# Seven block products for q, k, v and gates of seven sequences, and a first phase in three stages

## The chip, the cores and the metric

The kernel runs on one core of a Trainium2 chip. The metric is the device time of one execution in microseconds (us); a kernel's time is the median of its runs. Engines are named as the profile names them: PE is TensorE's matmul, PEld its weight load, DVE is VectorE, ACT is ScalarE, POOL is GpSimd, SP is SyncE, whose queue issues most DMAs.

## What is computed

Eight sequences of 1024 tokens of width 512, all float32. Cut to what matters:

```python
xn = layernorm(x)
q = xn @ Wq                                  # 512 -> 128
gate = softmax(xn @ Wg, axis=-1)             # 512 -> 3
for i in range(3):
    k, v = xn @ Wk[i], xn @ Wv[i]            # 512 -> 128 each
    w = decay[i] ** max(t_diff - 1, 0) * causal
    blended += gate[..., i:i+1] * ((q @ k.T * w) @ v)
s = blended @ Wo * out_scale
g = silu(ffn(xn))          # gate, up, down: weights lut[idx], 1376 wide inside
out = x + s * g
```

In the kernel's layout the causal mask runs backwards in time: a token attends to those behind it, so chunks of 128 tokens are worked from the last to the first, with a running state that decays from chunk to chunk.

## The kernel before, in words

It has two phases. Phase 1 (`phase_1`, to 604.8 us of the span) does the attention up to `blended` for each sequence, stores normalized tokens and sums of their blocks (`xs_d`) for phase 2, and builds the feed-forward weights from the table of 16 values (`ffn_weights`). Phase 2 is the feed-forward part, on weights and tokens that it loads back; its big products already go by seven products of blocks instead of eight, at two levels.

Phase 1 is written as Python generators that a loop steps by hand: for each sequence `b` eight steps `k`, each with three sections. `keep_order` (L26) then fixes that order for PE, DVE, ACT and POOL, so every engine works its instructions in the order in which they are traced; SP's queue is fixed only for the first steps. `tick` and `defer` put a DMA's issue some sections later. The generators:

- `project(b)`: for each of eight chunks load x (L335), statistics on ACT with a power on POOL (L350 to L353; on DVE for sequence 0, L343 to L347), normalize (L361 or L358), four transposes to `xnT` (`pt`, L366), copied by ACT (L367). Values and gate logits of a chunk are four matmuls of 387 columns (`pv`, L373); queries and keys of half a sequence are four times four matmuls of 512 columns (`pq`, L410). Each result is copied once by ACT (L376, L413). The softmax of the gates goes through DRAM (`gT_d`) and comes back broadcast to all partitions (`ga`). At the end DVE forms four sums of token blocks (`ts`, L467), and the features of the first half are still being made while the next sequence starts (`ending`).
- `chunks(b-1)`: for each chunk, from the last: keys are transposed (`pk`, L507) and scaled by ACT (`ks`, L510); `gated` multiplies gates and queries on DVE (`qa`, in place in `ga`, L491) and then by a decay table on POOL (`qb`, L495); scores (`psc`, L516), times the decay mask on DVE (`pr`, L518); state update (`pu`, L524) and output (`po`, L538), copied by ACT into `bl` (L539). The state is copied by ACT (L543) and scaled in PSUM (L550).
- `ffn_weights`: 16 jobs and more of a table lookup on DVE, 19 instructions on 1024 columns each (bits L197, index L200, leaves L204, selects L221), then block sums on POOL (L249 to L253, L267 to L273), then stores to `wgu_d`, `quad_d`, `wd_d`. The lookup's result lies in a tile `wgu` with two buffers: a job's first leaf (L204 `wgu<-`) waits until the job two before has let go of its buffer.

PSUM has eight banks: four in the pool `p_a` (`pt`, `pv`, `pq`), three in `p_c` (`pk`, `psc`, `po`), one in `p_r` (`pu`). A tile's buffer comes free when all that read it are done.

Within a step of the loop the order is: first section `pk` and its scalings, then `pt` and the statistics; second section `pq` and the softmax, then `gated`, `psc` and `pr`; third section `pv`, then `pu`, `po` and the state. `build_some` puts up to six pieces of `ffn_weights` (a piece is most often one VectorE instruction) between them.

Of the kernel before, what the change touches and what calls it, by code (L numbers as in the profile page):

```python
# [9 lines left out]
F32 = mybir.dt.float32  # L10
# [7 lines left out]
P = 128  # L18
# [19 lines left out]
def recurrent_block(ctx: ExitStack, tc, x, wq, wk, wv, wo, wg, decay_logits, out_scale, lut, gidx, uidx, didx, out):  # L38
# [18 lines left out]

    nc = tc.nc
# [12 lines left out]
    NQ = NO // 4  # L71
    EPS = 1e-5
# [20 lines left out]
    def more_weights(wvg_sb, wqk_sb):  # L93
        nc.scalar.dma_start(out=wvg_sb[:, :, NI * D :], in_=wg.rearrange("(c p) d -> p c d", p=P))
# [51 lines left out]
    def tables():  # L146
# [31 lines left out]
        for step, first in ((1, 0), (0, P)):  # L178
            back = small.tile([P, NI, P], F32, name="back", tag="back", bufs=2)
            nc.sync.dma_start(  # L180
                out=back, in_=bass.AP(pow_d.tensor, pow_d.offset + first, [[step, P], [2 * P, NI], [1, P]])
            )
            backs.append(back)
# [42 lines left out]
    def ffn_weights(build, pool, pair_pool):  # L226
# [5 lines left out]

        upper = []

        def gate_up(o):
# [19 lines left out]
            defer(3, lambda: nc.sync.dma_start(out=wgu_d[o], in_=wide))  # L255
            if o >= 2 * NK:
                return
            if o % 2 == 0:
                upper.append(w[:, 1:])
                return  # L260
            up, low = upper.pop(), w[:, 1:]
            to = quad_d[o // 4][:, :, o // 2 % 2, :].rearrange("p k (t m) -> p k t m", m=P)
            pair = pair_pool.tile([P, 7, 4, P], F32, name="pair", tag="pair")
            nc.sync.dma_start(out=to[:, :, 0:2, :], in_=up)
            defer(3, lambda: nc.sync.dma_start(out=to[:, :, 2, :], in_=low[:, :, 1, :]))
            b21, b22, b11, b12 = low[:, :, 0], low[:, :, 1], up[:, :, 0], up[:, :, 1]
            nc.gpsimd.tensor_tensor(pair[:, :, 0], b21, b22, ALU.add)  # L267
            yield
            nc.gpsimd.tensor_tensor(pair[:, :, 1], pair[:, :, 0], b11, ALU.subtract)
            yield  # L270
            nc.gpsimd.tensor_tensor(pair[:, :, 2], b11, b21, ALU.subtract)
            yield
            nc.gpsimd.tensor_tensor(pair[:, :, 3], b12, pair[:, :, 1], ALU.subtract)  # L273
            defer(4, lambda: nc.sync.dma_start(out=to[:, :, 3:7, :], in_=pair))
# [34 lines left out]

    def warm_up(n):  # L310

        warm = p_a.tile([P, P], F32, name="warm", tag="a")
# [3 lines left out]
    def project(b, pools, sides, kept):  # L316

        xp, xnp, tp, att = pools
        wvg_sb, wqk_sb = sides
        xnT = xnp.tile([P, NV, T], F32, name=f"xnT{b}", tag="xnT")
        mean, rstd, shift = (small.tile([P, NC], F32, name=f"{k}{b}", tag=k) for k in ("mean", "rstd", "shift"))
        v_sb = att.tile([P, NC, NI * D + NI], F32, name=f"v{b}", tag="v")
        gt = v_sb[:, :, NI * D :]
        qT, kT = {}, {}
        gates = []
        kept[b] = (v_sb, gates, qT, kT)  # L330
        xts = {}

        def load(c):
            xts[c] = xp.tile([P, V], F32, name=f"x{b}_{c}", tag="x")
            nc.sync.dma_start(out=xts[c], in_=x[b, ts(c, P), :])  # L335

        def statistics(c):

            m, r = mean[:, c : c + 1], rstd[:, c : c + 1]
            if b == 0:  # L340
                st = small.tile([P, 6], F32, name=f"st{b}_{c}", tag="st")
                mv = small.tile([P, 2], F32, name=f"mv{b}_{c}", tag="mv")
                nc.vector.bn_stats(st, xts[c])  # L343
# [4 lines left out]
            else:  # L348
                junk = small.tile([P, V], BF16, name=f"junk{b}_{c}", tag="junk", bufs=1)
                nc.scalar.activation(junk, xts[c], AF.Copy, scale=-1.0 / V, accum_out=m)  # L350
                nc.scalar.activation(junk, xts[c], AF.Square, bias=m, accum_out=r)  # L351
# [3 lines left out]
        def normalize(c):  # L355
# [757 lines left out]
```

## Time and profile before

| | |
|---|---|
| median of 3 runs | 2160.95 us (2160.52 to 2160.99) |
| the profiled execution's own time | 2158.71 us |
| its span, first to last instruction | 2156.9 us |
| granted TensorE clock | 1.000 |
| first matmul of phase 2's products (L687) | 608.3 us |
| transposes of sequences 0 to 7 begin at | 6.0, 46.3, 120.5, 194.8, 270.7, 344.9, 419.1, 493.3 us |
| DMA | 316.8 MB, 147 GB/s over the span |

How to read the page: "busy" is the time in which an engine had an instruction under way, "xcount" the number of instructions. A group's line has the source line, the engine and operation, the tiles as out<-in, the shape, the count, then busy time and the mean of one in ns, then the engine's idle time just before them with what ended it. In the timeline each line is a run of like instructions: start, length, engine, line, tiles, shape, count, and in brackets the idle time before with its releaser. The view by windows gives, for a stretch of time, its length and the busy time of PE, PEld, DVE, ACT and POOL with their counts, then the granted clock, DMA share and GB/s.

### The profile page before, as it was taken

Reading aid. Unit: us, or ns where it says so; the run is one execution under the profiler, and the core shown is the slowest. Engines: PE = TensorE matmul, PEld = TensorE weight load, DVE = VectorE, ACT = ScalarE, POOL = GpSimd, SP = SyncE. Lnnn points to the kernel's source line nnn. Section 1 sums busy time; section 2 is a strip of 40 time slices with the busy share of each in tenths; the row PEclk is TensorE's granted clock in tenths of the full one; section 3 lists DMA queues with packets and bytes.
Section 4 is the critical chain, followed back from the end, with each engine's and each line's share of the span. In section 5 each row is a group of like instructions: output and inputs, shape, how many; then the busy total and the mean of one; then the engine's idle time right before and its main releaser. Section 6 shows DMA issues by size and latency. Waiting matters only on the chain.

```text
span 2156.9 us, 26203 instructions
## 1 busy us (share of the span) xinstructions
PE 2147.4 (100%) x9486; PEld 1647.1 (76%) x9486; DVE 1158.4 (54%) x1701; ACT 863.9 (40%) x1900; POOL 979.8 (45%) x902
## 2 busy tenths in 40 slices
PE   9999999999999999999999999999999999999998
PEld 5666666666668778778878887887788688778876
DVE  6888687678645435534543453354345435533543
ACT  3666666666334214413431441243144124413521
POOL 2554545444244553634455452455435353634442
PEclk9999999999999999999999999999999999999999
DMA  8776654545374434434442443345244334434411
GB/s 193 192 196 177 205 199 153 186 147 162 114 297 154 145 106 150 141 115 138 150 155 96 145 149 117 130 154 169 75 152 149 130 117 154 129 119 149 156 57 54
DMA packets 145943, 316.83 MB, mean 147 GB/s; under 512 B 50867, under 2 KB 76214, under 8 KB 144790
## 3 DMA queue, kind: packets, MB, share of 16 engines
q1 hardware_dynamic: 135974, 290.50, 41.7%
q0 software_dynamic: 7728, 23.86, 3.0%
q8 instruction: 75, 1.23, 0.2%
q10 hardware_dynamic: 2112, 0.79, 0.1%
q14 instruction: 54, 0.44, 0.1%
HBM read 233.98 MB, written 81.14 MB: 146 GB/s over the span
## 4 chain that ended last, share of the span: by engine, by line
PE 98%; POOL 1%; issue 0%; ACT 0%; DVE 0%; DMA 0%; POOLq 0%
PE s L737 32%; PE ds L976 22%; PE pq L410 10%; PE pv L373 8%; PE sE L737 5%; PE fs L687 4%; PE po L538 4%; PE ds L987 2%; PE ps L998 2%; PE psc L516 2%; PE pu L524 2%; PE fsE L687 2%; PE pt L366 1%; PE pk L507 1%; PE sE L780 1%; PE s L780 1%
## 5 line engine op out<-in xcount | busy, mean ns | idle before, releaser
L737 PE MATMUL s<-xs,wq 128*128 128x256 f32 x3192 | 715.1, 379 | 0.0
L737 PEld LDWEIGHTS s<-xs,wq 128*128 128x128 f32 x3192 | 605.6, 190 | 94.1 <-issue 7.0
L976 PE MATMUL ds<-wd,s 128*128 128x256 f32 x1280 | 286.7, 379 | 0.0
L976 PEld LDWEIGHTS ds<-wd,s 128*128 128x128 f32 x1280 | 243.2, 190 | 33.1
L410 PE MATMUL pq<-xnT,wqk_sb 128*128 128x512 f32 x512 | 230.3, 592 | 0.0
L976 PE MATMUL ds<-wd,h 128*128 128x256 f32 x960 | 222.9, 379 | 0.0
L976 PEld LDWEIGHTS ds<-wd,h 128*128 128x128 f32 x960 | 182.3, 190 | 52.5 <-issue 27.1
L831 POOL TENSOR_TENSOR u<-u,e 128x512 f32<-128x512 f32 x64 | 79.8, 1268 | 276.1 <-DVE u L827 276.1
L760 DVE TENSOR_TENSOR s<-s,e 128x512 f32<-128x512 f32 x133 | 93.0, 700 | 202.2 <-ACT s L759 202.2
L373 PE MATMUL pv<-wvg_sb,xnT 128*128 128x387 f32 x512 | 177.5, 488 | 0.0
L1001 POOL TENSOR_TENSOR gx<-gx 128x512 f32<-128x512 f32 x63 | 80.3, 1274 | 184.3 <-DVE gx L999 183.6
L410 PEld LDWEIGHTS pq<-xnT,wqk_sb 128*128 128x128 f32 x512 | 92.4, 190 | 92.1 <-issue 91.8
L764 DVE TENSOR_TENSOR sE<-s,e 128x512 f32<-128x512 f32 x133 | 93.0, 699 | 102.6 <-PE s L737 102.6
L737 PE MATMUL sE<-xs,wq 128*128 128x256 f32 x532 | 136.5, 379 | 0.0
L352 POOL TENSOR_SCALAR rstd<-rstd 128x1 f32<-128x1 f32 x56 | 26.8, 479 | 238.2 <-ACT junk L351 237.6
L373 PEld LDWEIGHTS pv<-wvg_sb,xnT 128*128 128x128 f32 x512 | 92.7, 190 | 54.3 <-issue 1.9
L755 ACT COPY e<-sE 128x512 f32<-128x512 f32 x133 | 77.8, 585 | 136.1 <-PE sE L737 136.1
L671 POOL TENSOR_TENSOR xs<-xs 128x1792 f32<-128x1792 f32 (+1 forms) x38 | 127.9, 3380 | 1.0
L1017 ACT ACTIVATE gx<-ds 128x256 f32<-128x256 f32 x32 | 12.3, 383 | 285.9 <-PE ds L987 285.9
L759 ACT COPY s<-s 128x512 f32<-128x512 f32 x133 | 75.8, 570 | 96.6 <-PE s L737 96.6
L748 ACT COPY s<-s 128x512 f32<-128x512 f32 x133 | 75.8, 570 | 95.8 <-PE s L737 92.1
L737 PEld LDWEIGHTS sE<-xs,wq 128*128 128x128 f32 x532 | 101.1, 190 | 13.7
(169 smaller groups left out, 3298.2 us busy)
## 6 DMA issues: line engine op xcount, KB each, us to landing
wq<-quadd SPq DMA_DIRECT2D x112, 896.0 KB, 4.4
xs<-xsd SPq DMA_DIRECT2D x8, 3584.0 KB, 11.9
wq<-quadd SPq DMA_DIRECT2D x42, 448.0 KB, 3.8
x<-in_x SPq DMA_DIRECT2D x64, 256.0 KB, 5.9
xsd<-ts SPq DMA_DIRECT2D x8, 2048.0 KB, 7.0
gx<-in_x SPq DMA_DIRECT2D x64, 256.0 KB, 2.7
out<-gx POOLq DMA_DIRECT2D x63, 256.0 KB, 2.3
ga<-gTd SPq DMA_DIRECT2D x16, 768.0 KB, 4.9
```

Source lines behind the costliest of these rows:

```text
L373: nc.tensor.matmul(pv, lhsT=xnT[:, v, ts(c, P)], rhs=wvg_sb[:, v, :], start=(v == 0), stop=(v == NV - 1))
L410: nc.tensor.matmul(pq, lhsT=wqk_sb[:, v, ts(j, D)], rhs=xnT[:, v, ts(hf, U)], start=(v == 0), stop=(v == NV - 1))
L538: nc.tensor.matmul(po, lhsT=lh, rhs=rh, start=(n == 0), stop=(n == len(prods) - 1))
L671: nc.gpsimd.tensor_tensor(o, x1, x2, ALU.subtract)
L687: nc.tensor.matmul(ps, lhsT=w[:, 2 * W_OF[k] + n, :m], rhs=xs[:, X_OF[k], 2 * n : 2 * n + 2, :], start=start and n == 0, stop=stop and n == 1,
L737: nc.tensor.matmul(self.t[n][:, ts(a, H)], lhsT=self.w[:, a, (0, 1, 6, 2, 3, 4, 5)[i - 1], :], rhs=self.xs[:, X_OF[self.ks[a]], D_OF[i], : ...
L755: nc.scalar.copy(self.e, self.t[3])
L760: nc.vector.tensor_tensor(self.t[1], self.t[1], self.e, ALU.add)
L764: nc.vector.tensor_tensor(self.t[3], self.t[2], self.e, ALU.add)
L831: nc.gpsimd.tensor_tensor(o[:, n], o[:, n], other[:, n], ALU.add)
L976: nc.tensor.matmul(ps, lhsT=lhs[k][:, n, :], rhs=wd_sb[n][:, ts(D_OF[k], H)], start=start and n == 0, stop=stop and n == NK - 1, skip_grou ...
L1001: (nc.vector if end else nc.gpsimd).tensor_tensor(g, g, xr, ALU.add)
```

## The change

For sequences 1 to 7, values with gates and queries with keys are computed by seven products of blocks in place of eight (`nodes`), from four sums of token blocks and four sums of weight blocks. The value weights are padded from 387 to 388 columns and cut in two halves of 194 (`HG`). Each of four nodes a sequence (two for values, each with products of four matmuls of 194 columns, two for queries and keys, each with products of two matmuls of 512) has four PSUM roles with a bank each (`p_a` now has one buffer for each of four tags); a product is added to what ACT copied into the bank. One product is one piece of the generator; a node takes two steps, with one, two and one piece in the sections of the even step and one and two in the odd one. Sequence 0 keeps the plain products (`plain`), in 12 steps instead of 8.

Phase 1 becomes three generators, a sequence apart: `tokens` (load, statistics, normalize, transposes; sequence 1 as well as 0 on DVE; `pt` in `p_c` from sequence 1 on), `nodes`, and `chunks`. `sums_of_tokens` makes the four token sums at the end of the step before a sequence's nodes, two on DVE, two on POOL, in one buffer; `keep_tokens` stores them in step 1. `gated`'s first multiplication goes to POOL, except in the last sequence. `bl` is stored chunk by chunk. In `ffn_weights` the sums of a pair are written into the pair's own tiles, the stores of single tiles that nobody loads go away, and the order of sums in `quad_d` changes with the index in `Node.product`. x is loaded four chunks ahead with five buffers (six before).

The diff, cut to its core:

```diff
 def gate_up(o):
-            defer(3, lambda: nc.sync.dma_start(out=wgu_d[o], in_=wide))
+            if o >= 4 * NQ:
+                defer(3, lambda: nc.sync.dma_start(out=wgu_d[o], in_=wide))
...
-            pair = pair_pool.tile([P, 7, 4, P], F32, name="pair", tag="pair")
-            nc.sync.dma_start(out=to[:, :, 0:2, :], in_=up)
-            defer(3, lambda: nc.sync.dma_start(out=to[:, :, 2, :], in_=low[:, :, 1, :]))
-            nc.gpsimd.tensor_tensor(pair[:, :, 0], b21, b22, ALU.add)
-            yield
-            nc.gpsimd.tensor_tensor(pair[:, :, 1], pair[:, :, 0], b11, ALU.subtract)
-            yield
-            nc.gpsimd.tensor_tensor(pair[:, :, 2], b11, b21, ALU.subtract)
-            yield
-            nc.gpsimd.tensor_tensor(pair[:, :, 3], b12, pair[:, :, 1], ALU.subtract)
-            defer(4, lambda: nc.sync.dma_start(out=to[:, :, 3:7, :], in_=pair))
+            pair = pair_pool.tile([P, 7, P], F32, name="pair", tag="pair")
+            nc.gpsimd.tensor_tensor(pair, b11, b21, ALU.subtract)
+            if o >= 4 * NQ:
+                for _ in range(6):
+                    yield
+            nc.gpsimd.tensor_tensor(b21, b21, b22, ALU.add)
+            yield
+            nc.gpsimd.tensor_tensor(b11, b21, b11, ALU.subtract)
+            yield
+            nc.gpsimd.tensor_tensor(b12, b12, b11, ALU.subtract)
+            defer(2, lambda: nc.sync.dma_start(out=to[:, :, 4:6, :], in_=up))
+            defer(3, lambda: nc.sync.dma_start(out=to[:, :, 2:4, :], in_=low))
+            defer(3, lambda: nc.sync.dma_start(out=to[:, :, 6, :], in_=pair))
...
+    def tokens(xp, xnp):
...
+            pool, tag = (p_c, "c") if b else (p_a, next_role())
+            pt = pool.tile([P, NV, P], F32, name=f"pt{b}_{c}", tag=tag)
...
+    def sums_of_tokens(tp, b):
+        tss[b] = ts_ = tp.tile([P, 4, 2, U], F32, name=f"ts{b}", tag="ts")
+        b11, b12, b21, b22 = blocks_of_x(xnTs[b])
+        t1, t2, t3, t4 = (ts_[:, k] for k in range(4))
+        nc.vector.tensor_tensor(t1, b12, b11, ALU.subtract)
+        nc.vector.tensor_tensor(t2, b22, t1, ALU.subtract)
+        nc.gpsimd.tensor_tensor(t3, b22, b12, ALU.subtract)
+        nc.gpsimd.tensor_tensor(t4, b21, t2, ALU.subtract)
...
+    def nodes(b, sides, att, kept):
...
+        def node(name, product, shape, c11, c12, c21, c22):
+            pa, pb, pe, pc = (p_a.tile([P] + shape, F32, name=f"{r}{name}", tag=r) for r in ROLES)
+            product(pa, 1, True)
+            nc.scalar.copy(pb, pa)
+            yield
+            product(pe, 5, True)
+            nc.scalar.copy(c21, pe)
+            yield
+            product(pb, 6, False)
+            nc.scalar.copy(pc, pb)
+            nc.scalar.copy(c12, pb)
+            yield
+            product(pa, 2, False)
+            nc.scalar.copy(c11, pa)
+            yield
+            product(pc, 7, False)
+            nc.vector.tensor_tensor(c22, pc, c21, ALU.add)
+            yield
+            product(pe, 3, False)
+            nc.vector.tensor_tensor(c12, pe, c12, ALU.add)
+            yield
+            product(pc, 4, False)
+            nc.scalar.copy(c21, pc)
+            yield
...
+            def product(ps, k, start):
+                for a in range(2):
+                    for v in range(2):
+                        nc.tensor.matmul(
+                            ps[:, a, :],
+                            lhsT=xk[k][:, v, ts(2 * n + a, P)],
+                            rhs=wv_k[k][:, v, :],
...
+            def product(ps, k, start):
+                for v in range(2):
+                    nc.tensor.matmul(
+                        ps,
+                        lhsT=wq_k[k][:, v, ts(n, D)],
+                        rhs=xk[k][:, v, :],
...
 def gated(c):
-            nc.vector.tensor_tensor(qa, qa, qT[hf][:, ts(k, P)].unsqueeze(1).to_broadcast([P, NI, P]), ALU.mult)
+            eng = nc.vector if at_end else nc.gpsimd
+            eng.tensor_tensor(qa, qa, qT[hf][:, ts(k, P)].unsqueeze(1).to_broadcast([P, NI, P]), ALU.mult)
...
 def phase_1():
+            for k in range(NC + NC // 2):
+                two = k == NC - 1 or k > NC
+                tick()
+                some(fresh, 3)
+                next(setup, None)
+                if k == NC:
+                    sums_of_tokens(tp, 0)
+                some(weights, k > 0)
+                next(more, None)
+                tick()
+                next(first)
+                some(weights, k >= NC // 2)
+                some(fresh, 3 * two)
+                some(weights, 2 * (k >= NC // 2))
+                tick()
+                next(first)
...
+            sums_of_tokens(tp, 1)
+            for b in range(1, B + 1):
+                older = chunks(b - 1, (chk, blp), kept)
+                newer = nodes(b, sides, att, kept) if b < B else iter(())
                 for k in range(NC):
                     tick()
                     next(older, None)
+                    next(fresh, None)
+                    some(weights, 2)
                     next(newer, None)
+                    if k == 1 and b < B:
+                        keep_tokens(b)
                     tick()
                     next(older, None)
+                    next(fresh, None)
+                    some(weights, 2 * (b < B))
+                    some(newer, 2)
                     tick()
+                    next(fresh, None)
                     next(older, None)
+                    if k == NC - 1 and b + 1 < B:
+                        sums_of_tokens(tp, b + 1)
+                    some(weights, 2 * (b < B))
+                    some(newer, 1 - k % 2)
...
 def product(self, n, i, start=False):
...
-                            lhsT=self.w[:, a, (0, 1, 6, 2, 3, 4, 5)[i - 1], :],
+                            lhsT=self.w[:, a, (0, 1, 5, 3, 2, 4, 6)[i - 1], :],
```

## The prediction

> **What bounds the kernel now.** I read the page's busy rows first, then the groups, then TensorE's timeline in the first phase.
>
> ```profile
> PE 2147.4 (100%) x9486; PEld 1647.1 (76%) x9486; DVE 1158.4 (54%) x1701; ACT 863.9 (40%) x1900; POOL 979.8 (45%) x902
> L410 PE MATMUL pq<-xnT,wqk_sb 128*128 128x512 f32 x512 | 230.3, 592 | 0.0
> L373 PE MATMUL pv<-wvg_sb,xnT 128*128 128x387 f32 x512 | 177.5, 488 | 0.0
> ```
>
> A busy PE row says little by itself, since matmul ends are modelled. The timeline says more; this is one chunk step of the fourth sequence:
>
> ```profile
> 317.07 0.49 PE L507 MATMUL pk<-ident,kT 128*128 128x128 f32 x3
> 317.40 0.60 PE L366 MATMUL pt<-ident,x 128*128 128x128 f32 x4
> 317.84 3.60 PE L410 MATMUL pq<-xnT,wqk_sb 128*128 128x512 f32 x8
> 321.27 0.83 PE L516 MATMUL psc<-ga,kT 128*128 128x128 f32 x6
> 321.94 2.77 PE L373 MATMUL pv<-wvg_sb,xnT 128*128 128x387 f32 x8
> 324.55 0.83 PE L524 MATMUL pu<-v,ks 128*128 128x128 f32 x6
> 325.22 0.83 PE L538 MATMUL po<-qb,R 128*128 128x128 f32 x6
> 325.89 0.83 PE L538 MATMUL po<-pr,v 128*128 128x128 f32 x6
> ```
>
> Each run starts one pitch after the last start of the run before, without a gap. A run's length less its last matmul's mean gives the pitch: (3.60-0.592)/7 = 0.430 us at 512 columns, (2.77-0.488)/7 = 0.326 at 387, (0.83-0.275)/5 = 0.111 at 128. A matmul of the program is two records here. So phase 1 (to 604.8 us) is TensorE's from 8 us on; its stages take 74.2 us each. What TensorE saves there is time, unless a wait comes in its place.
>
> **What the products save.** Values: 64 records of 387 columns become 112 of 194 (two nodes, seven products, four matmuls, two records). At 194, between the rows of 128 and 387, a record takes 0.111+66/259x0.215 = 0.166 us. So 64x0.326 = 20.9 becomes 112x0.166 = 18.6: 2.3 saved. Queries and keys: 64 records of 512 become 56: 27.5 less 24.1, 3.4 saved. Seven sequences: 7x5.7 = 40.0 us.
> A rule speaks against it: the Trainium skill, "TensorE: Matmul & The Clock Gate", "Back-to-back issue gap", has weight load and matmul set the spacing together, about 81 ns at 128 columns and 131 at 512. Interpolated, values would go from 64x115 to 112x90 ns, 2.7 us dearer, features 1.0 cheaper: the change would add 7x1.7 = 12 us. The rows here rise with the columns (0.111, 0.326, 0.430), so I take the saving of 40.0.
>
> **Copies and adds of the nodes.** A node has six ScalarE copies and two VectorE adds for four copies before. Copies: 24 instead of 16 a sequence, 0.4 to 0.47 us each by ScalarE's starts in the timeline, 4 us of a 68.5 us stage. ScalarE is busy 47 to 50 us of a 75 us stage; 54 of 68.5 fits. The tightest wait is pb, copied after product 1 and added to by product 6. On ScalarE it stands behind last step's end (blend, state, three scalings), three key scalings and the token copy, 3.6 us after the step's start; product 6 starts at 4.1 (pk, pt, product 1, psc, product 5). Cover 0.4 us: priced at 0, at most 0.3 x 14.
> VectorE: adds +5.0, two token subtractions to GpSimd -2.6, gating to GpSimd -5.0 a sequence. It has 49 to 64 us of work in a 75 us stage now, and keeps room. GpSimd gets gating (8x1.1 us) and two subtractions (2x2.6): 36 to 41 in the early stages becomes about 52 of 68.5. The shares fit; the order is the trouble.
>
> **The first sequence (+12.8).** Its stage gets four more steps and tokens of two sequences, both normalized on VectorE.
>
> ```profile
> 0.00:46.00 46.00, 43.92 (x163) 26.82 (x164) 30.45 (x70) 14.82 (x31) 11.86 (x22) 1.00 0.79 171
> 347.00:423.00 76.00, 76.00 (x367) 50.99 (x366) 48.82 (x73) 50.27 (x134) 35.47 (x35) 1.00 0.53 182
> ```
>
> (Columns: PE, PEld, DVE, ACT, POOL busy.) VectorE ended its lookups of this stage at 41.4 us. With tokens 8 to 10 begun (statistics 1.09, normalize 0.46) it ends step 7 at about 44.6. Steps 8 to 11 hold 8.2 of tokens, 14.4 of lookups (16 steps), 2.5 for the first sequence's sums, 0.8 of softmax, about 1.3 of waits for GpSimd: 71.8. TensorE has only 8 transposes and four feature runs there, 46.0+3.5+13.8 = 63.3, and each transpose waits for VectorE. Then t1 and t2 of sequence 1 (2.4), t4 on GpSimd (2.7), and, behind t4 in GpSimd's order, the first gating (1.1): psc can start at 78.1. TensorE alone would be there at 65.3. No shape here is new; between 8 and 16 by the lookups' length.
>
> **Six transitions (+20.4).** `sums_of_tokens` of the next sequence comes at a stage's end; its one buffer is free only when the last product (4) has read it. From that end: t1 and t2 to 2.6, t4 to 5.5, gating to 6.7. A 1024-wide subtraction takes 1.26 us on VectorE (L467); on GpSimd 896 wide takes 2.3 (lines below), so 2.6. TensorE needs until psc: po 1.34, pk 0.33, pt 0.44, product 1 1.33: 3.4. It waits 3.3 to 3.4, and psc stands ahead of everything. The weight sums and gating of other steps can make it 6; none of it if the subtractions started earlier. 6x3.4 = 20.4.
>
> **Five pairs of weight tiles (+17.5).**
>
> ```profile
> 230.89 2.56 POOL L267 TENSOR_TENSOR pair<-wgu 128x896 f32<-128x896 f32 x1
> 233.52 2.42 POOL L269 TENSOR_TENSOR pair<-pair,wgu 128x896 f32<-128x896 f32 x1
> 235.89 2.46 POOL L271 TENSOR_TENSOR pair<-wgu 128x896 f32<-128x896 f32 x1
> 238.31 2.10 POOL L273 TENSOR_TENSOR pair<-wgu,pair 128x896 f32<-128x896 f32 x1
> 236.76 0.56 DVE L518 TENSOR_TENSOR pr<-psc,w_tab 128x384 f32<-128x384 f32 x1 [0.40 <-PE psc L516]
> 240.45 1.46 DVE L204 TENSOR_SCALAR wgu<-idx,lut_x,lut_sb 128x1024 int32<-128x1024 int32 x1 [3.14 <-POOL pair L273]
> ```
>
> The next tile's first leaf reuses the buffer that the pair's upper tile leaves, and waits for GpSimd's last read. Now GpSimd writes into that tile, and a store of 896 KB (1 KB pieces) follows its last subtraction: the leaf waits for the landing too. Stores of that size land in 4.0 (wgud) to 12.5 us (quadd from wgu); I take 6. The leaf is also one step earlier (1.4 us) and the last subtraction about 2 later for gating: VectorE stands 7 to 9 us more. Behind it stand pr, for which po waits, and the node's add, for which product 4 waits. Their room is about 5 us: from psc's end, product pair 2.6 to 3.4, pu 0.7, and some lead. I take 3.5 a pair, 5x3.5 = 17.5; between 0 (landing in 4, leaf late) and 8 each.
>
> **Smaller edits.** Chunks alone in the last stage: 3.2 us a step in the trace (592.5 to 602.0), of which 3.0 is pitch; four more such steps, 0.6. The wide stores of eight tiles go, 7 MB; blends are stored in eight pieces and tokens in four; nothing on TensorE waits for them. SP's order puts gate reads and loads of x (now four ahead) behind these stores, with more than a step's room: 0, up to 5. Phase 2 keeps its instructions: 0.
>
> **Sum.** 2158.7 (the profiled execution's own time) -40.0 +12.8 +20.4 +17.5 +0.6 = 2170.0. The median of the runs, 2160.95, is 2.2 above it: 2172.
>
> **Rivals.**
> 1. The waits are covered (not slower). Subtractions of the next sequence need not wait for product 4, or GpSimd's backlog is small, and landings fall in VectorE's idle time (1.7 us a step before pr, 106 us in phase 1). Then only the first stage is lost: 2158.7-40.0+12.8+0.6+2.2 = 2134. For it: VectorE waits for TensorE at most steps. Against: one buffer and one order. It decides as soon as transitions and pairs together cost under 27 us. Chance 0.20.
> 2. Transitions cost, pairs do not: 2134+20 = 2155, at the edge of no change. 0.17.
> 3. VectorE becomes the bound: each pair costs 8, and products wait for its adds: 2172+22 = 2194 or more. 0.10.
> 4. The change doesn't shorten the products: a record cannot be shorter than its weight load's 0.190 us row. Values then cost 21.3, and 7x3.0 = 21 are saved: 2191. Against it, psc runs at 0.111 with the same loads. 0.03.
> The forecast's own case has 0.50 and spans 2160 to 2185.
>
> A run of this kernel can be told from no change by about 0.2%, 4.3 us. Faster than 2156.6: rival 1 and half of rival 2, 0.29. Within: the rest of 2 and the low end of the forecast, 0.14. Slower: 0.57. The range leaves out the lowest of rival 1 and the end of 3: 2136 to 2193.
>
> **What would show it.** Runs of four v records 0.166 apart, and 56 of 512 a sequence. At each stage's first psc an idle TensorE of 3 to 6 us, ended by GpSimd's gating; near 65 to 78 us one ended by VectorE's normalize, then gating. Five first leaves with waits of 7 us or more ended by a DMA. I am wrong if those gaps are under 1 us, or if waits lie inside the nodes (product 6 on ScalarE, 4 on VectorE).

## The result and the profile after

| | before | after |
|---|---|---|
| median | 2160.97 us (2160.52 to 2164.84) | 2229.55 us (2226.18 to 2230.93, 4 runs) |
| the profiled execution's own time | 2158.71 us | 2228.99 us |
| its span; clock | 2156.9 us; 1.000 | 2227.2 us; 0.982 |
| first psc of sequence 0's chunks | 50.2 us | 98.85 us |
| first psc of sequence 7's chunks | 570.9 us | 643.4 us |
| end of phase 1 (first zs) | 604.8 us | 675.0 us |

The ratio is 1.0311 [1.0293, 1.0329]: 68.6 us slower, where 11 were forecast. All of it is in phase 1, which is 70.2 us longer in the profiles.

The products did what was forecast. From TensorE's timeline of after, the end of the fourth sequence's stage and the start of the next:

```profile
327.71 1.88 PE L621 MATMUL peq<-xnT,wqs 128*128 128x512 f32 x4
...
333.52 1.48 PE L600 MATMUL pav<-wvg_sb,xnT 128*128 128x194 f32 x8
347.52 1.65 PE L674 MATMUL psc<-ga,kT 128*128 128x128 f32 x6 [12.52 <-POOL ga L649]
```

The pitch is (1.48-0.33)/7 = 0.165 us at 194 columns (forecast 0.166), and (1.88-0.592)/3 = 0.43 at 512. The counts in phase 1 are 784 records of 194 columns and 392 of 512, seven times 112 and 56. By pitch and count the 40 us are there, so phase 1 got some 110 us of waits and slow work instead: TensorE stands 86.2 us of it, against under 4 in before, and most of the rest is work at half clock (below). The last line has both: psc stands 12.5 us for a multiplication on GpSimd, and then takes 1.65 us instead of 0.83. The page's busy row of after, its clock row (40 slices of 55.7 us, in tenths of full speed) and psc's group:

```profile
PE 2135.3 (96%) x9766; PEld 1698.1 (76%) x9766; DVE 1196.0 (54%) x1690; ACT 868.7 (39%) x1901; POOL 1088.1 (49%) x975
PEclk9799998999999999999999999999999999999999
L674 PE MATMUL psc<-ga,kT 128*128 128x128 f32 x384 | 58.8, 293 | 51.0 <-POOL ga L649 50.6
```

TensorE is busy 96% instead of 100%, GpSimd 1088 us instead of 980. The clock row falls under nine tenths in the second and the seventh slice, both in phase 1 (a 9 is 90% or more, so smaller losses don't show). The waits of TensorE in after (us in total, times, longest); in before the first of these rows does not exist and the longest wait is 1.4 us:

```profile
PE psc L674 <- POOL ga L649: 50.6, 9, 12.5
PE pt L391 <- DVE x L379: 16.2, 3, 7.5
PE pu L682 <- ACT ks L668: 5.5, 1, 5.5
PE pt L391 <- ACT x L382: 2.9, 1, 2.9
PE pbq L621 <- ACT pbq L571: 2.9, 3, 1.4
PE pcv L600 <- DVE v L584: 2.5, 2, 1.5
```

Why is gating so late? The two timelines of the last transition in after, VectorE's and then GpSimd's:

```profile
565.72 3.42 DVE L473 TENSOR_TENSOR ts<-xnT 128x1024 f32<-128x1024 f32 x1 [0.30 <-issue]
569.18 1.23 DVE L474 TENSOR_TENSOR ts<-xnT,ts 128x1024 f32<-128x1024 f32 x1
...
571.50 4.22 DVE L207 TENSOR_SCALAR leaf<-idx,lut_x,lut_sb 128x1024 int32<-128x1024 int32 x2
```

```profile
565.71 2.35 POOL L475 TENSOR_TENSOR ts<-xnT 128x1024 f32<-128x1024 f32 x1 [11.13 <-PE pcq L621]
570.54 3.23 POOL L476 TENSOR_TENSOR ts<-xnT,ts 128x1024 f32<-128x1024 f32 x1 [2.48 <-DVE ts L474]
573.73 2.85 POOL L649 TENSOR_TENSOR ga<-ga,qT 128x384 f32<-128x384 f32 x2
```

t1 on VectorE and t3 on GpSimd start together. t3 takes 2.35 us; t1 takes 3.42, which is t3's 2.35 and 1.07 more, about what such a sum needs alone (t2, right behind it, with GpSimd idle, takes 1.23). Then t4 takes 3.23 us beside VectorE's work, and two leaves that take 0.81 us each elsewhere take 4.22 together. By these durations (those of GpSimd are rough in this profile) an engine waits for the other's whole instruction. The forecast had 1.26 and 2.6 us side by side. From product 4's end at 565.7 to psc at 575.2 the chain takes 9.5 us, with no weight sums in the queue; the forecast had 6.7.

In the fourth transition (the 12.5 us above) GpSimd had more in its queue; its timeline in after:

```profile
331.78 2.95 POOL L271 TENSOR_TENSOR pair<-wgu 128x896 f32<-128x896 f32 x1
334.81 2.94 POOL L275 TENSOR_TENSOR wgu<-wgu 128x896 f32<-128x896 f32 x1
337.70 2.34 POOL L475 TENSOR_TENSOR ts<-xnT 128x1024 f32<-128x1024 f32 x1
340.00 2.34 POOL L476 TENSOR_TENSOR ts<-xnT,ts 128x1024 f32<-128x1024 f32 x1
342.30 2.07 POOL L277 TENSOR_TENSOR wgu<-wgu 128x896 f32<-128x896 f32 x1
344.44 2.07 POOL L279 TENSOR_TENSOR wgu<-wgu 128x896 f32<-128x896 f32 x1
346.47 1.95 POOL L649 TENSOR_TENSOR ga<-ga,qT 128x384 f32<-128x384 f32 x2
```

The four subtractions of a weight pair stand around the token sums, all ahead of the gating that psc waits for. VectorE's second token sum beside them:

```profile
332.82 2.99 DVE L474 TENSOR_TENSOR ts<-xnT,ts 128x1024 f32<-128x1024 f32 x1
```

It takes 1.91 us until GpSimd's first subtraction ends at 334.73, and 1.08 more: the same sum as in the last transition.

By windows of after (length, busy PE, PEld, DVE, ACT, POOL, clock, DMA share, GB/s), the first sequence's stage against the 46 us shown of before, and one slow window:

```profile
0.00:44.00 44.00, 42.64 (x157) 26.88 (x158) 31.07 (x78) 11.15 (x22) 10.55 (x23) 1.00 0.73 159
44.00:100.00 56.00, 29.58 (x91) 16.88 (x90) 40.65 (x58) 14.77 (x34) 37.89 (x29) 0.75 0.77 220
...
338.20:351.90 13.70, 4.38 (x16) 4.38 (x17) 2.69 (x4) 0.11 (x1) 13.30 (x11) 0.50 0.66 207
```

From 44 to 100 us TensorE works 29.6 of 56 us. The second reading is the clock: 0.75 there, 0.50 in the window that begins inside the wait. There are ten such stretches of 3.4, 6.8 or 13.7 us at 0.50 in phase 1, each at a stall, 78.5 us in all with 42.3 of TensorE's work in them: an estimate from this is that half of that work, 21 us, is the halving.

### The profile page after: what moved, and what is told of

It reads as the page before. It is cut to its first block, busy times and chain, and to the rows that moved or that the text cites. A ratio compares the mean times of both kernels' runs of the same rounds, so it can differ in the third digit from the quotient of the medians.

```text
span 2227.2 us, 27197 instructions
## 1 busy us (share of the span) xinstructions
PE 2135.3 (96%) x9766; PEld 1698.1 (76%) x9766; DVE 1196.0 (54%) x1690; ACT 868.7 (39%) x1901; POOL 1088.1 (49%) x975
## 3 DMA queue, kind: packets, MB, share of 16 engines
q8 instruction: 77, 1.26, 0.3%
## 4 chain that ended last, share of the span: by engine, by line
PE 88%; POOL 4%; DVE 4%; DMA 2%; issue 1%; ACT 1%; SPq 0%; POOLq 0%; DVEq 0%; ACTq 0%
PE s L918 31%; PE ds L1157 22%; PE sE L918 5%; PE fs L868 4%; PE po L696 3%; PE ds L1168 2%; PE ps L1179 2%; PE pcq L621 2%; PE paq L621 2%; PE peq L621 2%; PE psc L674 2%; PE fsE L868 2%; PE pu L682 1%; PE pev L600 1%; DVE leaf L207 1%
## 5 line engine op out<-in xcount | busy, mean ns | idle before, releaser
L207 DVE TENSOR_SCALAR leaf<-idx,lut_x,lut_sb 128x1024 int32<-128x1024 int32 (+2 forms) x119 | 113.7, 983 | 0.0
L918 PEld LDWEIGHTS sE<-xs,wq 128*128 128x128 f32 x532 | 101.1, 190 | 13.7
L1190 DVE TENSOR_TENSOR pw<-ds,pw 128x256 f32<-128x256 f32 x32 | 13.6, 425 | 177.0 <-PE ds L1157 177.0
L1016 POOL TENSOR_TENSOR h<-h,e 128x512 f32<-128x512 f32 x64 | 80.0, 1274 | 57.5 <-issue 46.4
L674 PE MATMUL psc<-ga,kT 128*128 128x128 f32 x384 | 58.8, 293 | 51.0 <-POOL ga L649 50.6
L674 PEld LDWEIGHTS psc<-ga,kT 128*128 128x128 f32 x384 | 54.8, 204 | 67.6 <-POOL ga L649 53.9
```

The costliest lines, as they stand in the source:

```text
L207: nc.vector.tensor_scalar(o.bitcast(I32), iv, lut_x[:rows, k, :], lut_i[:rows, k, 0:1], ALU.bitwise_and, ALU.bitwise_xor,)
L674: nc.tensor.matmul(psc[:, i, :], lhsT=kc[:, i, :], rhs=qa[:, i, :], start=True, stop=True)
L918: nc.tensor.matmul(self.t[n][:, ts(a, H)], lhsT=self.w[:, a, (0, 1, 5, 3, 2, 4, 6)[i - 1], :], rhs=self.xs[:, X_OF[self.ks[a]], D_OF[i], : ...
L1016: nc.gpsimd.tensor_tensor(of_h(half, n), of_h(half, n), two(other[:, n]), ALU.mult)
```

## The experiments

Times are medians; the kernel before, run beside each, took 2159.6 to 2160.8 us. "psc" is the first psc of sequence 0's chunks, which TensorE's own work would allow at 65.3 by the prediction's estimate. Its time has a scatter of its own: SP issues the first read of gates, which waits for a store of gates to land and has loads of x behind it, at 43.1 us in after and at 39.3 to 42.9 in the fifteen runs built on it, in e2, e3 and e4 before the edit can act. A psc a few us earlier in one trace shows nothing by itself.

**Which queue does psc wait in?** My theory at first was order alone: gating stands behind t4.

e1, gating of a sequence's first chunk traced ahead of the token sums:

```diff
             following = gated(NC - 1)
+            yield
...
+                    if k == NC - 1 and b < B:
+                        coming = chunks(b, (chk, blp), kept)
+                        next(coming)
```

> The changed kernel, with the first gating of a chunk pass traced before the token sums of the next sequence, not behind them; nothing is left out. Theory (the order on GpSimd): the first psc of a stage waited 50.6 us in seven stages because its gating stood behind t3, t4 and what was queued there. Now the gating is done a step's third section earlier, so these waits fall under 1 us each, the clock stays at 1.0 at those places, and 2229.6 becomes 2165 to 2180. Rival (GpSimd is simply too full): the wait moves on to t4, so that product 7 or 4, or the next gating, waits instead: 2210 or more, with waits of 3 us and more inside the nodes.

2215.24 us, ratio 1.0262 [1.0245, 1.0279]. The theory missed; the time is the rival's, though the waits came at po and not inside the nodes. The waits of TensorE:

```profile
PE psc L675 <- POOL ga L649: 21.7, 7, 8.1
PE po L697 <- DVE pr L677: 15.9, 4, 5.6
```

Some 29 of 50.6 us of psc's wait are gone, and po, whose pr stands on VectorE behind the token sums, waits 15.9 where it waited 1.3; gating still stands behind weight pairs elsewhere. Order was a part of it only.

e5, e1 with gating on VectorE, as in before; e6, e5 with t3 and t4 on VectorE too:

```diff
-            eng = nc.vector if at_end else nc.gpsimd
-            eng.tensor_tensor(qa, qa, qT[hf][:, ts(k, P)].unsqueeze(1).to_broadcast([P, NI, P]), ALU.mult)
+            nc.vector.tensor_tensor(qa, qa, qT[hf][:, ts(k, P)].unsqueeze(1).to_broadcast([P, NI, P]), ALU.mult)
```
```diff
-        nc.gpsimd.tensor_tensor(t3, b22, b12, ALU.subtract)
-        nc.gpsimd.tensor_tensor(t4, b21, t2, ALU.subtract)
+        nc.vector.tensor_tensor(t3, b22, b12, ALU.subtract)
+        nc.vector.tensor_tensor(t4, b21, t2, ALU.subtract)
```

> As e1_gate_first, and the gating multiplication (L649) is back on VectorE in every sequence; nothing is left out. e1 (2215.2) moved the wait from the first psc to later gatings behind the pair sums on GpSimd (8.1 us once) and to pr on VectorE (15.9 us). Theory: both come from GpSimd's added work, first as a queue (gating behind 13 us of weight and token sums), then through VectorE, whose two-input work slows while GpSimd runs (a token subtraction 2.15 us in place of 1.31). With gating gone from GpSimd, psc's waits for it go, VectorE's lookups get shorter, and the time falls to 2180 to 2195. Rival (VectorE is the bound, and takes 56 more instructions): pr and the node adds come later still, and the time stays within 8 us of 2215 or rises.

> As e5_gate_dve, and the third and fourth token sum are on VectorE too; nothing is left out. Theory (contention): alone on VectorE the four sums take 4 x 1.22 us, hardly more than the two that took 4.3 beside GpSimd's, so VectorE loses at most 1 us a transition, GpSimd gains 5, and the time is 3 to 10 us under e5. Rival (VectorE's own work counts): the sums stand before pr, po waits 2 us more at each of six transitions, and the time is 5 to 15 us over e5.

e5: 2207.81 us, 1.0225 [1.0209, 1.0240], only 7 below e1: psc's wait is gone, but po waits 17.4 us for pr and the products 15.0 for VectorE's adds. e6: 2183.66, 1.0111 [1.0096, 1.0126], 24 us below e5, more than expected. It gives VectorE 16 instructions more. These are the groups of token sums of e5 and then e6 (busy, mean ns):

```profile
L476 POOL TENSOR_TENSOR ts<-xnT,ts 128x1024 f32<-128x1024 f32 x8 | 23.6, 2948 | 13.9 <-DVE ts L474 13.9
L475 POOL TENSOR_TENSOR ts<-xnT 128x1024 f32<-128x1024 f32 x8 | 20.4, 2548 | 18.5 <-PE pcq L621 18.3
L473 DVE TENSOR_TENSOR ts<-xnT 128x1024 f32<-128x1024 f32 x8 | 18.7, 2334 | 1.4 <-issue 1.4
```

```profile
L473 DVE TENSOR_TENSOR ts<-xnT 128x1024 f32<-128x1024 f32 x8 | 12.1, 1516 | 1.6 <-issue 1.6
L475 DVE TENSOR_TENSOR ts<-xnT 128x1024 f32<-128x1024 f32 x8 | 11.6, 1454 | 0.0
```

By windows VectorE is busy 519 us of phase 1 with 16 instructions more, against 528 in e5: what it takes over costs it less than sharing did. Gating is not on GpSimd in either run, and in e5 the products wait 1.0 us for a sum on GpSimd, so the 24 us are hardly a matter of GpSimd's queue; they speak for the two engines slowing each other.

e11, this last edit alone on after. 

> The changed kernel with all four token sums on VectorE, gating still on GpSimd and behind them in the traced order; nothing is left out. Theory: the first psc of a stage waits because t4 stands before gating on GpSimd; with the sums on VectorE gating no longer waits for them, and psc's 50.6 us fall under 15. VectorE's sums run alone. e6 gained 24 us over e5 by the same edit; here 20 to 35: 2195 to 2210. Rival (GpSimd's weight sums hold the gating up just as well): psc still waits 25 us or more, and the time stays above 2215.

2200.41 us, 1.0183 [1.0168, 1.0199]: 29 us less than after from two lines, as expected. psc's wait for gating fell from 50.6 to 19.3 us in three places, not quite under the theory's 15. So the two sums on GpSimd cost most of what the transitions lost. This edit alone doesn't part the two ways in which they did it, since it takes two instructions out of gating's queue as well; e5 to e6 does.

**Single parts on the kernel before.** e7 takes the new weight pairs (the diff of `gate_up` and `Node.product`'s order), e8 gating on GpSimd:

```diff
-            nc.vector.tensor_tensor(qa, qa, qT[hf][:, ts(k, P)].unsqueeze(1).to_broadcast([P, NI, P]), ALU.mult)
+            eng = nc.vector if at_end else nc.gpsimd
+            eng.tensor_tensor(qa, qa, qT[hf][:, ts(k, P)].unsqueeze(1).to_broadcast([P, NI, P]), ALU.mult)
```

> The kernel before with the changed weight pairs alone (sums in place, stores of whole tiles, no single stores), nothing left out. The prediction gave five pairs 17.5 us (0 to 40), since the next first leaf waits for a store. In the changed kernel VectorE waited 11.3 us for it at three pairs, and TensorE little. Theory: VectorE's room before pr takes it up: 0 to 6 us slower than before (2160 to 2166). Rival (the prediction): 15 us or more slower.

> The kernel before with the gating multiplication on GpSimd (but for the last sequence) alone; nothing is left out. Theory: GpSimd's pair bursts of 12 to 14 us now delay a gating that psc needs a step later: psc waits 3 to 8 us at each of five bursts, with the clock's dips on top: 15 to 45 us slower (2175 to 2205). Rival (gating has a whole step's room, and only the token sums at the transitions harm): under 6 us slower.

e7: 2170.03 us, 1.0049 [1.0034, 1.0064], 10.5 us slower for the pairs, between the two theories. VectorE's first leaves in it, and before's only row of the kind, which is not a transfer's:

```profile
DVE wgu L204 <- DMA quadd<-wgu: 12.4, 4, 5.5
```
```profile
DVE wgu L204 <- POOL pair L273: 7.3, 2, 4.1
```

e8: 2174.39 us, 1.0065 [1.0048, 1.0082], 14.8 us slower, just under the theory's range: psc waits 10.1 us for gating in six places, and gating takes 1.35 us on GpSimd against 0.63 on VectorE.

**Smaller suspects, each on after.** e2 puts seven useless products behind the first product of a stage, into a bank that product 5 overwrites; e3 gives the blends four buffers for two; e4 leaves out weight pieces in the first sequence's last four steps (they come later).

```diff
+            if name[0] == "v" and name[-1] == "0":
+                for _ in range(7):
+                    nc.tensor.matmul(
+                        pe, lhsT=ident, rhs=wo_sb[:, : 2 * HG].rearrange("p (a h) -> p a h", a=2), start=True, stop=True
+                    )
```
```diff
-            tc.tile_pool(name="blp", bufs=2) as blp,
+            tc.tile_pool(name="blp", bufs=4) as blp,
```
```diff
-                some(weights, k > 0)
+                some(weights, 0 < k < NC)
...
-                some(weights, k >= NC // 2)
+                some(weights, NC // 2 <= k < NC)
...
-                some(weights, 2 * (k >= NC // 2))
+                some(weights, 2 * (NC // 2 <= k < NC))
```

> The changed kernel plus seven useless matmuls of 388 columns (4.6 us) after the first product of each of the seven stages, in the place where TensorE idles before psc; nothing is left out. Theory: the idle stretches also cost clock: the granted clock drops to 0.5 in windows of 3.4 to 13.7 us from them on, and work done in them takes double. With the place filled the clock stays at 1.0 at most transitions, and 8 to 12 us go: 2218 to 2222. Rival (the low clock falls only into the idle stretch, and costs nothing): no change, or up to 4 us slower where a stall is shorter than the filler: 2228 to 2234.

> The changed kernel with four buffers for the piecewise blend copies in place of two; nothing is left out. Theory: ScalarE waits 18 us in all for a blend store to land (7.8 us once in the last stage, where the store queues behind the loads of phase 2), and the key scalings and pu stand behind it. With four buffers that pu wait of 5.6 us and its slow clock go: 2229.6 becomes 2219 to 2224. Rival (SP's queue is late anyway): the wait only comes two chunks later, and the time stays within 3 us.

> The changed kernel without the lookup pieces in steps 8 to 11 of the first sequence; they are all worked later, the last of them beside and after the last chunk pass; nothing is left out. Theory (VectorE bounds the end of the first stage by its lookups): 14 us of lookups go from the path there, the first psc comes at 83 to 88 us in place of 98.9, and the time falls by 8 to 14 us less what the 16 pieces cost at the end. Rival (the loads of x, one buffer fewer, and the weight sums on GpSimd bound it): psc comes at 94 or later, and the time falls by under 4 us or rises.

e2: 2220.93 us, 8.6 less than after with more work: the half-clock stretches shrink from 78.5 to 48 us, the clock rises from 0.982 to 0.989. So the clock is a cost of its own, but a smaller one than 8.6: the two profiles differ by 5.8 us, and 2.8 of these are the earlier first psc (96.0), most of it scatter ahead of the first filler. From the first psc to the last the stages are 3.0 us shorter. e3: 2219.17, 10.4 less, and the 5.5 us of pu are gone. Of this, 3.3 us in its profile is scatter ahead of the first psc, where no blend buffer is in use yet, and 7.2 is the last stage; ScalarE's line of after there is

```profile
655.20 0.27 ACT L698 COPY bl<-po 128x128 f32<-128x128 f32 x1 [7.84 <-DMA bld<-bl]
```

a copy that waits for the store of the blend two chunks before, with the scaled keys of the next chunk behind it. e4: 2216.09, 13.5 less; psc at 91.45 instead of 98.85, not the 83 to 88 expected. Its first read of gates is issued at 39.4 us, 3.7 earlier than in after, so about half of the 7.4 us at psc can be scatter: lookups are a part of the first stage's loss at most.

**The first sequence's stage.** e10, sequence 1 normalized on ScalarE, as before had it:

```diff
-            if s < 2 * NC:
+            if s < NC:
```

> The changed kernel with statistics and normalization of sequence 1 on ScalarE, as those of sequences 2 to 7; nothing is left out. Theory (VectorE bounds steps 7 to 11 of the first sequence): 12 us of its work go, the transposes no longer wait for it, the first psc comes at 84 to 90 in place of 98.9, and 2229.6 becomes 2215 to 2221. Rival (the loads of x, behind 3.6 MB of token stores, and GpSimd's sums bound that stage): psc comes at 94 or later, and under 5 us are gained.

2229.14 us: nothing gained, the rival's result. ScalarE's normalize waits 9.4 us for a power on GpSimd, which stands behind t3, t4 and weight sums; pt waits 12.7 us there. So GpSimd holds this stage too once VectorE's part is gone. e9 therefore takes e6 with e10's edit, e3's buffers and six empty pieces behind each pair:

```diff
-            for _ in range(3):
+            for _ in range(6):
                 yield
```

> e6_gate_sums_dve (2183.7) with three more edits: sequence 1 is normalized on ScalarE (as e10), four blend buffers (as e3), and three more empty pieces behind each pair, so that the store lands while no lookup waits for it; nothing is left out. Theory (each wait has its own cause, and they add): 8 to 14 us of the first stage, 6 to 10 of the last, 4 to 8 at the pairs: 2152 to 2166, about the kernel before. Rival (VectorE is now the bound, busy 558 of 630 us of phase 1): what is taken away in one place comes back as po and product waits in another: 2168 to 2178.

2161.61 us, 1.0003 [0.9995, 1.0011]: the whole loss is gone (22 us below e6; which of the three edits gave how much was not parted), but psc comes at 86.3. VectorE is busy 519 of 630 us of phase 1 in e6 by windows; the 558 of the expectation is the sum of durations that overlap. Of the two next tries, e12 (e9, the read of that sequence's second half of gates deferred by 13 sections for 6) missed since the read stayed ahead of four loads of x in SP's order, so the theory stayed untried. e13 (e12, weight sums on VectorE, t3 and t4 behind the first psc of their own stage) took waits of po for pr away (14.3 us to 3.9) and put others in their place (5.5 for adds of the nodes, 4.9 for qb).

```diff
-                half = softmax(att, 0, v_sb, gates, 0, NC // NHALF, [(0, 6)])
+                half = softmax(att, 0, v_sb, gates, 0, NC // NHALF, [(0, 13)])
```
```diff
-            nc.gpsimd.tensor_tensor(s1, a21, a22, ALU.add)
+            nc.vector.tensor_tensor(s1, a21, a22, ALU.add)
...
+    def more_sums(b):
...
+        nc.vector.tensor_tensor(t3, b22, b12, ALU.subtract)
+        nc.vector.tensor_tensor(t4, b21, t2, ALU.subtract)
...
+                    if k == 0 and b < B:
+                        more_sums(b)
```

> e9_four_fixes (2161.6) with the read of the first sequence's second gate half issued 13 sections after its write in place of 6; nothing is left out. Theory (SP's queue): in the first stage SP stood from 61.4 to 71.3 us at that read, which waits for the landing of the gate write, and the loads of x stood behind it; so the transposes of steps 10 and 11 waited 7 us, and VectorE's work or GpSimd's was not what held them (e10 gained nothing). The first psc comes at 74 to 80 us in place of 86.3, the time is 2150 to 2156. Rival (GpSimd's powers, behind the weight sums, bound the tokens): psc at 84 or later, 2158 or more.

> As e12_read_later, the weight sums on VectorE, and the third and fourth token sum of a sequence a section later (behind the first psc of its own stage); nothing is left out. Theory: the powers no longer wait behind 11 us of weight sums on GpSimd (2 to 5 us in the first stage), and pr of a stage's first chunk comes 2.4 us earlier, so that po's waits of about 2 us at seven transitions go: 6 to 14 us under e12: 2140 to 2148. Rival (VectorE has no room left): the sums hold up pr, the node adds and the clock one step later, and the time is within 4 us of e12.

2161.78 us, 1.0011 [1.0003, 1.0020], and 2159.62, 1.0000 [0.9991, 1.0008]; psc at 84.25 and 85.5: both theories missed. e15 and e16 keep SP's order as traced, on e13 and on after with e12's edit:

```diff
-                if k == 3:
-                    keep_order(tc, seen, (mybir.EngineType.SP,))
...
+                    if (b, k) == (1, 2):
+                        keep_order(tc, seen, (mybir.EngineType.SP,))
```

> e13_sums_spread (2159.6) with SP's order pinned to the traced one up to the second step of sequence 1's stage; nothing is left out. In e12 and e13 the scheduler still put the late gate read ahead of four loads of x: SP stood from 60.9 to 69 or 71 us at it, so e12 did not try what it was meant to. Here the loads stand ahead of the read. Theory (SP's queue bounds the first stage): the first psc comes at 72 to 79 us in place of 85.5, and the time is 2146 to 2154, under both kernels. Rival (statistics, powers on GpSimd and normalization, one token after the other, bound it): psc stays at 83 or later, the time within 3 us of 2159.6.

> The changed kernel with the late gate read and the pinned SP order of e15 alone; nothing is left out. Theory: VectorE's waits for loads of x in steps 7 to 11 (9 us) go, and the first psc comes 3 to 8 us earlier than 98.9: 2220 to 2226, less than in e15 since VectorE's lookups and GpSimd's sums stand next. Rival (the queue alone bounds the stage): psc at 88 or earlier, 2218 or less.

2167.72 us, 1.0034 [1.0022, 1.0047], and 2235.96, 1.0351 [1.0335, 1.0367]. Both missed. SP no longer stood at a read, and yet the x load landed late. The windows of e15 say why (the last two columns are DMA share and GB/s):

```profile
50.00:60.00 10.00, 6.82 (x25) 3.62 (x24) 7.63 (x13) 8.27 (x20) 7.44 (x10) 0.92 1.04 412
60.00:70.00 10.00, 4.94 (x13) 2.19 (x12) 8.25 (x10) 4.10 (x9) 2.30 (x3) 0.84 0.90 65
```

From 50 to 60 us token stores fill the DMA engines. From 60 to 70 us they are 90% busy and move 65 GB/s. In this stretch lies the write of 1536 gates as single words of four bytes (15.8 us from issue to landing), and the x load for which TensorE waits 8.8 us was issued right behind it. The words themselves are soon through: the trace has 1568 packets of under 512 B from 60 to 62 us, 9 ns each. What is slow are the pieces of 2 KB behind them; these are 181 of the 202 packets from 62 to 70 us, and the engines are 80% busy there:

```profile
DMA packets 202, 0.37 MB, mean 46 GB/s; under 512 B 21, under 2 KB 21, under 8 KB 202
```

By the trace such a piece takes 84 ns in the mean from 50 to 52 us and 600 ns from 62 to 70. Why is open; whether the write brings it can be tried. e18 and e17 defer this write by 11 sections for 2, and its read by 18, on e13 with SP's order kept through the first stage (e18), and on e15 (e17):

```diff
-        defer(2, write)
+        defer(11 if (b, hf) == (0, 0) else 2, write)
...
-                half = softmax(att, 0, v_sb, gates, 0, NC // NHALF, [(0, 13)])
+                half = softmax(att, 0, v_sb, gates, 0, NC // NHALF, [(0, 18)])
...
+            keep_order(tc, seen, (mybir.EngineType.SP,))
             coming = chunks(0, (chk, blp), kept)
```

> The kernel with sums and gating on VectorE, four blend buffers and token sums t3 and t4 behind the first scores, with SP's order kept as traced through the first sequence's stage and the write of that sequence's second half of gates (single words of four bytes) nine sections later, behind the x loads of sequence 1. Theory (that write held up the x load for which the transposes at 64.6 us waited 8.6 us): this wait is under 2 us, the first psc is at 75 to 79 us and the time 2150 to 2155 us. Rival (the next thing in line, the rstd on GpSimd or the token stores, takes its place): first psc at 83 us or later and a time within 3 us of 2160.

> The same, with SP's order kept as traced through two steps of sequence 1's stage as well. Theory: 8 us less than 2168, 2157 to 2162 us, with the first psc at 75 to 79 us. Rival: first psc at 83 us or later, a time within 3 us of 2168.

e18: 2152.83 us, 0.9964 [0.9951, 0.9976]; e17: 2159.86, 0.9996 [0.9988, 1.0004], 7.9 below e15. psc is at 77.8 and 78.8. Both as the theory had it, and e18 is faster than both kernels. From e15 to e17 nothing but this write and its read moves; e18 has SP's order changed with it. What TensorE still waits for in it:

```profile
PE pt L391 <- ACT x L382: 9.9, 4, 3.2
PE pcv L604 <- DVE v L588: 5.8, 5, 3.0
PE po L700 <- POOL qb L656: 4.9, 3, 1.6
PE po L700 <- DVE pr L680: 4.0, 5, 1.3
```

Its seven stages take 492.3 us from the first psc to the last, against 520.8 in before. About 12 us in the first stage stay lost, most of them where transposes wait for normalized x (9.9 us). That e17 is 7 us above e18 (psc 1.0 us later, one more wait of 3.3 us for an add, at 109 us, and a stage of 73.7 us instead of 68.8) comes with the longer fixed order of SP; which transfer does it stays open.

## Why the prediction was wrong, by its steps

The direction and the place were right (first psc of each stage, ended by GpSimd's gating, and first leaves ended by a DMA); the size was wrong by 58 us.

- **Products, -40.0: right.** The pitches stand, and the rule on the issue gap does not hold for these rows (0.165 us at 194 columns, where the step interpolated 0.09 from it), as the step had it.
- **Six transitions, +20.4: the step that failed.** Waits of psc behind the first stage come to 50.6-7.35 = 43.3 us: 42.0 at the six transitions (4.5 to 12.5 each, forecast 3.4) and 1.2 in two later steps. The step took each duration as if an engine were alone and allowed "6" with a backlog. In the last transition t1 and t4 took 3.4 and 3.2 us for 1.26 and 2.6, gating 1.4 for 1.1; in others the pairs' subtractions stood in the same queue. e6's 24 us and e11's 29 show the first, the fourth transition's timeline the second. The Trainium skill, "SBUF — State Buffer", "SBUF: two separate sides", says that a VectorE instruction with two SBUF inputs and a GpSimd instruction that reads SBUF hold the shared port in turn, for a whole instruction each. The rows agree (3.42 = 2.35+1.07 and 2.99 = 1.91+1.08). By that rule t1 behind t3, t2, t4 and gating, from a stage's end, come to an estimate of 3.6+1.26+2.6+1.1 = 8.6 us instead of 6.7, before any backlog; so the rule alone gives 11 of the 21.6 us missing at six transitions.
- **"VectorE keeps room", "the shares fit; the order is the trouble": wrong.** Work was moved to GpSimd and both engines got busier: over phase 1, by windows, VectorE is busy 504 us instead of 461 (the step had it 2.6 a sequence down) and GpSimd 376 instead of 261. e1 mended the order and gained 14 us; taking work back gained more.
- **First sequence, +12.8: mis-sized.** psc came at 98.9 instead of 78.1, 20.8 us more. The step followed VectorE alone and priced GpSimd's part at 1.3 us of waits; the sums of the weight blocks for the nodes, which are GpSimd's too and stand ahead of t3 until 93.2 us in after, are not in it at all. e10 shows GpSimd's power behind sums, e4 lookups in some part, e17 and e18 a transfer. Up to some 3 us are scatter. "SP's order: 0, up to 5" was wrong in kind: not SP's order but what the DMA engines were doing cost 7 to 8 us of psc (e13 to e18, e15 to e17).
- **The clock: a missing term.** An estimated 21 us of slow work, 8 of it in the first stage, by the windows; e2 shows that some of it is real (3.0 us behind the first stage). The Trainium skill, "TensorE: Matmul & The Clock Gate", "Part 1: The HAM clock gate", has half rate after an idle window of about 3.4 us; the stretches here are multiples of 3.4 us at 0.50 at stalls, but waits of 2.9 and 3.0 us, shorter than such a window, brought one too (after, near 89 us; e18, near 514). It was there to be used: 3.4 us was what I had for each wait.
- **Pairs, +17.5: too high.** Waits of first leaves for the store were 2.6, 6.5 and 2.1 us in after, not 7 to 9 at five places, and 10.5 us alone (e7).
- **"Nothing on TensorE waits" for blend stores: wrong** in the last stage, by 5.5 us of wait and 7.2 of that stage's time (e3).
- **Copies on ScalarE at 0: near.** pbq waits 2.9 us in all, and the products 4.3 for the adds on VectorE.

An estimate of the sum: beyond the forecast +20.8 (first stage, its slow clock within), +22.9 (transitions), +5.5 (blends), +13 (slow clock behind the first stage), +8.5 (small waits in nodes and at po), less what the pairs were overpriced. That is 70.7 less up to 17.5, so 53 to 71, where phase 1 ended 58.9 us later than forecast (675.0 instead of 616.1). The terms overlap and were not parted further.

What stays open: how much of the 13 is a cost (with only the sums moved, in e11, the same estimate gives 9: 18.2 us of work at half clock behind the first stage), and which part of the first stage's last 12 us is lookups.

## What to carry to other kernels

Work given to GpSimd beside VectorE is not priced by its own row: ask what VectorE runs at that moment, and count on the sum of the two durations where both read two tiles. Where TensorE is the bound and the change adds a stall of some 3 us or more, allow for half clock behind it (3.4 to 13.7 us here), in which the work takes double. A transfer's price is not its bytes: list what stands ahead of it on the DMA engines, with the pieces' size. And before a few us in one trace are put down to an edit, look whether they arise before the edit can act.

## What the runs showed of the hardware

- Token sums of 1024 columns on VectorE: t1 and t2 have means of 2.61 and 1.70 us in after, with t3 and t4 on GpSimd, and of 1.22 each in e18, with all four on VectorE (t3 and t4 1.60 and 1.28 there). The lookup's leaves read one tile only, and took up to 2.8 us in after for 0.81 in the median all the same.
- Half clock came in stretches of 3.4, 6.8 and 13.7 us at waits of 2.9 to 12.5 us. Of e18's four waits of 2.9 to 3.2 us two brought one and two did not.
- A write of 1536 words of four bytes took 15.8 us from issue to landing in e15. Its words took 9 ns each; the 2 KB pieces behind it took 600 ns in the mean (62 to 70 us) instead of 84 (50 to 52 us). Moving the write behind the loads of x gained 7.9 us (e15 to e17).
